# Attention masks moved from TensorE to GpSimd, and exact rounding moved next to its use, in a fused attention and mixture-of-experts kernel

## The chip, the cores and the metric

The kernel runs on one core of one Trainium2 chip. Five engines work side by side, each through its own queue in order: TensorE (PE in the profile; PEld is its weight loads), VectorE (DVE), ScalarE (ACT), GpSimd (POOL) and SyncE (SP, which here only issues DMAs). The metric is the device time of one execution in microseconds (us); less is better.

## The reference

`x` has shape (16, 256, 128): 4096 tokens of 128 channels. Everything is float32.

```python
xn = layernorm(x)                                   # eps 1e-5
Q, K, V = (relu(xn @ W + b) for W, b in ...)         # 16 heads of 8
scores = einsum('bqhd,bkhd->bhqk', Qh, Kh) / sqrt(8)
key_mask = sign(abs(sum(xn, -1)))                   # 0 where the row's sum is exactly 0
scores = where(key_mask == 0, NEG, scores)
scores = where(tril == 0, NEG, scores)              # causal
attn = softmax(scores) * query_mask                 # query_mask is key_mask for the rows
attn_out = gamma * norm(attn @ Vh + xn) + beta      # LayerNorm, eps 1e-8
h = rms_weight * xn * rsqrt(mean(xn**2) + 1e-6)
top 2 of softmax(h @ gate_w.T) over 8 experts, weights normalised to 1
moe = xn + sum over the two of weight * (w2 @ (silu(w1 @ h) * (w3 @ h)))
return x + attn_out + moe
```

The key mask asks whether a row of `xn` sums to exactly zero in float32. So the kernel has to round the quotient `(x - mean) / root` exactly as the reference does; this is what is called exact rounding below.

## The kernel before, in words

128 tokens lie in the 128 partitions of a tile; 32 such tiles form 8 blocks of 4 (`BT = 4`), a block being two sequences. The instructions of TensorE stand in the order in which the program issues them; those of the other engines are put in order by a scheduler, within what their data allow, and keep that order on the chip.

**Early work** (`prepared`, L1059) runs over three chunks of tokens: tiles 0 to 4, 4 to 16, 16 to 32. For each chunk `normed` (L317) makes the LayerNorm: subtract the mean on ACT (L325), square and scan on DVE (L332, L334), a Newton square root in small DVE steps, and `xn` on ACT (L361). `exact` (L385) then rounds block by block: it splits `xn` in a high and a low half (`qh` on DVE, `ql`), makes three products `p` on ACT (L407), adds them to a remainder `r` (L412, L417), corrects `y` (L421), sums each row in the reference's order (`lane_sum`), and writes `off_all` (1 where the row's sum is zero) and `on_all`. For the first chunk the additions run on DVE, for the others on POOL (`eng`). `logits` and `route` (L432) choose two experts a token and scatter rows and weights into `lists` by indirect DMAs from POOL (L536): 32 for the first route (tiles 0 to 16), 16 for each of two more. `planned` (L819) makes the table of expert tiles, 256 tokens each.

**Attention** runs over 16 units: 8 blocks times 2 groups of 8 heads (`r`). `projected(n)` (L569) makes Q, K and V of a block; `diag` (L579) takes `off_all` into K. For a unit u:

- `scores(u, part)`, three parts: S = Q K on TensorE, a causal mask added by a matmul with `cmask[:, 0]` (L648), the row maximum on DVE (L658, L666).
- `queries(u)`: the maxima are transposed (`top_ps`, L685) and put into the queries: Qs on DVE (L687), Qm on ACT (L690).
- `weights(u, part)`, three parts: W = K Qm, transposed scores less their maximum (L710); the causal mask added by a matmul of the identity with `cmask[:, 1]` (L723); exp on ACT (L731) into `e`.
- `values(u, b)`: O = V e on TensorE (L743, L754), then oT on ACT. `finish(u, b)`: transposed back (`o_ps`, L773), divided by the sums, into `y`.

S, W and the experts' A and G share six PSUM buffers; all other PSUM tiles (O, Y, hT, R, `top_ps`, `o_ps`, q, k, v) share two.

**The experts** (`experts`, L900) run over 36 tiles as a generator with four steps a tile: A and G of the first half (L952); Y of the tile before (L969); A and G of the second half; hT of the next tile and R of the one before, with two indirect DMAs into `places` from POOL (L989).

The loop at L1110 interleaves all this. Between the parts of a unit stands `fill`: up to three steps of early work, the next block's projections, 1.55 expert steps on average from unit 3 on, and a step of `rest` (the second LayerNorm of blocks that are done). It is called six times a unit. In the before kernel `queries(u + 1)` stands behind `values(u, 1)`, and before each block the loop drains early work until the next block is rounded (L1114). Behind the last unit run the expert tiles that are left, the last `rest`, and loads of `places` that are added to `y` and written out.

Of the kernel before, what the change touches and what calls it, by code (L numbers as in the profile page):

```python
# [26 lines left out]
def tile_attention_plus_moe(  # L27
# [55 lines left out]
    EARLY_STEPS, EXPERT_STEPS, EXPERTS_FROM = 3, 1.55, 3  # L83
# [55 lines left out]
    for to, src, eng in ((qb_in, bq, nc.scalar), (kb_in, bk, nc.scalar)):  # L139
# [17 lines left out]
    cmask = const.tile([P, 2, P], BF16, name="cmask")  # L157
    G.memset(cmask, 0.0)
    G.affine_select(
        cmask[:, 0, :], cmask[:, 0, :], [[-1, P]], ALU.is_ge, MASKED, base=0, channel_multiplier=1  # L160
    )
    G.affine_select(
        cmask[:, 1, :], cmask[:, 1, :], [[1, P]], ALU.is_ge, MASKED, base=0, channel_multiplier=-1
# [153 lines left out]
    def normed(t0, t1):  # L317
# [60 lines left out]
        ninv = small.tile([P, nt], F32, tag="ninv", name=f"ninv_{n}")  # L378
        V.reciprocal(ninv, root)
        V.tensor_scalar(ninv, ninv, -1.0, None, ALU.mult)  # L380
        rhi, rlo = high_low(root[:], nt, "quot")
        roots[t0] = rhi, rlo, ninv
        yield

    def exact(c0, t0, t1, eng):  # L385

        rhi, rlo, ninv = roots[c0]
        n = f"x{t0}"  # L390
        for b in range(t0, t1, BT):
            bs = slice(b, b + BT)
            q, d = xn[:, bs, :], y[:, bs, :]
            i0 = b - c0
            qh = norm.tile([P, BT, C], F32, tag="qh", name=f"qh_{b}")
            ql = norm.tile([P, BT, C], F32, tag="ql", name=f"ql_{b}")
            r = norm.tile([P, BT, C], F32, tag="r", bufs=2, name=f"r_{b}")
            V.tensor_scalar(
                qh.bitcast(U32), q.bitcast(U32), HI_BITS, None, ALU.bitwise_and
            )  # L400
            eng.tensor_tensor(ql, q, qh, ALU.subtract)
            ps = []
            for k, (half, by) in enumerate(((qh, rlo), (ql, rhi), (ql, rlo))):
                p = norm.tile([P, BT, C], F32, tag=f"p{k}", name=f"p{k}_{b}")
                for t in range(BT):
                    i = i0 + t
                    S.activation(p[:, t, :], half[:, t, :], AF.Copy, scale=by[:, i : i + 1])  # L407
                ps.append(p)
            yield
            for t in range(BT):  # L410
                i = i0 + t
                V.scalar_tensor_tensor(  # L412
                    r[:, t, :], qh[:, t, :], rhi[:, i : i + 1], d[:, t, :], ALU.mult, ALU.subtract
                )
            yield
            for p in ps:
                eng.tensor_tensor(r, r, p, ALU.add)  # L417

            for t in range(BT):
                i = i0 + t  # L420
                V.scalar_tensor_tensor(  # L421
                    d[:, t, :], r[:, t, :], ninv[:, i : i + 1], q[:, t, :], ALU.mult, ALU.add
                )
            yield
        tot = small.tile([P, t1 - t0], F32, tag="tot", name=f"tot_{n}")
        yield from lane_sum(tot, y[:, t0:t1, :], t1 - t0, f"s{n}", V)
        V.tensor_scalar(off_all[:, t0:t1], tot, 0.0, None, ALU.is_equal)
        V.tensor_scalar(on_all[:, t0:t1], off_all[:, t0:t1], -1.0, 1.0, ALU.mult, ALU.add)
        exact_upto[0] = t1 // BT
        yield  # L430
# [138 lines left out]
    def projected(n):  # L569
# [6 lines left out]
        diag = qkv.tile([P, BT, P], BF16, tag="diag", name=f"diag_{n}")  # L576
# [4 lines left out]
        for r in range(NR):  # L581
            kp = misc(f"k_ps_{n}_{r}")
            T.matmul(kp, lhsT=wk_sb[:, r, :], rhs=xnT, start=True, stop=False)
            T.matmul(
                kp,
                lhsT=off_rows,
                rhs=diag.rearrange("p t k -> p (t k)"),
                start=False,
                stop=True,
            )  # L590
            KT = qkv.tile([P, BW], F32, tag="KT", bufs=3, name=f"KT_{n}_{r}")
            S.activation(KT, kp, AF.Relu, bias=kb_sb[:, r : r + 1])

            KTm = qkv.tile([P, HG, BW], F32, tag="KTm", bufs=2, name=f"KTm_{n}_{r}")
            V.tensor_scalar(KTm[:, 0, :], KT, head_mask[:, 0:1], None, ALU.mult)
            S.activation(KTm[:, 1, :], KT, AF.Copy, scale=head_mask[:, 1:2])
            yield
            qp = misc(f"q_ps_{n}_{r}")
            T.matmul(qp, lhsT=wq_sb[:, r, :], rhs=xnT, start=True, stop=True)
            QT = qkv.tile([P, BW], F32, tag="QT", bufs=2, name=f"QT_{n}_{r}")  # L600
            S.activation(QT, qp, AF.Relu, bias=qb_sb[:, r : r + 1], scale=QSCALE)
            state[n, r] = (QT, KT, KTm)
            yield
        for b in range(2):
# [16 lines left out]
    def scores(u, part):  # L621
# [21 lines left out]
        for g in range(NG):  # L643
            if part == 2:
                out = sp[g].rearrange("p (a k) -> p a k", k=P)
            else:
# [4 lines left out]
                rhs=cmask[:, 0, :].unsqueeze(1).to_broadcast([P, 4 if part == 2 else 2, P]),  # L651
# [5 lines left out]
            if part == 2:  # L657
                V.tensor_reduce(  # L658
# [5 lines left out]
                )  # L664
            else:
                V.tensor_reduce(  # L666
# [5 lines left out]
                )  # L672
# [20 lines left out]
    exps = {}  # L693

    def weights(u, part):
# [6 lines left out]
        for g in range(NG):  # L702
            rows = slice(32 * g, 32 * g + 32)
            for b in range(2) if part == 0 else (part - 1,):
                if part == 0:
                    out = sp[g][:, ts(b, SEQ)].rearrange("p (j q) -> p j q", j=HG)
                else:
# [7 lines left out]
                    stop=False,  # L715
                    skip_group_check=True,
                )
        for g in range(NG):
            if part == 0:
                out = sp[g].rearrange("p (a q) -> p a q", q=P)  # L720
            else:
                out = sp[g].rearrange("p (j q) -> p j q", j=HG)[:, :, 0:P]
            T.matmul(  # L723
                out,
                lhsT=ident_bf,
                rhs=cmask[:, 1, :].unsqueeze(1).to_broadcast([P, 4 if part == 0 else 2, P]),
                start=False,
                stop=True,
                skip_group_check=True,
            )  # L730
            S.activation(e[:, g, :], sp[g], AF.Exp)  # L731
# [327 lines left out]
    def prepared():  # L1059

        routed = 0
        for a, z in CHUNKS:
            eng = V if a == 0 else G
            yield from normed(a, z)

            first = min(a + BT, z) if a < 2 * BT else a
            if first > a:
                yield from exact(a, a, first, eng)
# [10 lines left out]
            for b in range(first, z, 2 * BT):  # L1079
                yield from exact(a, b, min(b + 2 * BT, z), eng)  # L1080

    exact_upto = [0]
    early_work = prepared()
    side = {"experts": iter(()), "rest": iter(()), "next": iter(())}
    due = [0.0]

    def fill(k_next=1):

        for _ in range(EARLY_STEPS):
            if next(early_work, None) is PAUSE:  # L1090
                break
        for _ in range(k_next):
# [12 lines left out]
    for _ in projected(0):  # L1105
        pass
# [3 lines left out]
    for u in range(len(units)):  # L1110
        n, r = units[u]
        more = u + 1 < len(units)
        if r == 0 and n + 1 < NB:
            while exact_upto[0] < n + 2:  # L1114
                next(early_work)
            side["next"] = projected(n + 1)
# [3 lines left out]
        fill()  # L1120
        if more:
            if r == 1:
                while (units[u + 1]) not in state:
                    next(side["next"])
            scores(u + 1, 0)
        fill()
        weights(u, 1)
        fill()
        if more:
            scores(u + 1, 1)  # L1130
        fill(r)
# [3 lines left out]
        fill(r)  # L1135
        weights(u, 2)
        finish(u, 0, o0)
        fill(r)
        if r == 1:
            for _ in side["next"]:  # L1140
                pass
        o1 = values(u, 1)
        if more:
            queries(u + 1)
        exps.pop((u, 0))
        finish(u, 1, o1)
# [91 lines left out]
```

## Time and profile before

| | us |
|---|---|
| median of 3 runs (lowest to highest) | 728.03 (725.95 to 730.34) |
| the profiled execution | 728.52 |
| its span, first to last instruction | 726.7 |
| TensorE busy | 566.6 (78%) |
| VectorE busy | 459.8 (63%) |
| ScalarE busy | 324.2 (45%) |
| GpSimd busy | 251.3 (35%) |
| W masks on TensorE (L723), busy | 41.8 |
| exact rounding's additions on GpSimd (L401, L417), busy | 37.0 |

In lines of groups, the columns are: source line, engine, operation, output <- inputs by the program's names, partitions x elements, count; then busy us and mean ns of one; then the engine's idle time before them and what ended it. In timelines: start, length, engine, line, operation, and in brackets the engine's idle time before it. In tables of stages: busy us of each engine with its number of instructions, the granted TensorE clock as a share of full speed, the share of the DMA engines and GB/s.

### The profile page before, as it was taken

To read this page: it belongs to the slowest core of one execution; us is meant where nothing else is said; L and a number is where in the kernel's file an instruction comes from. 1 tells how busy PE (TensorE), PEld (TensorE's weight loads), DVE (VectorE), ACT (ScalarE), POOL (GpSimd) and SP (SyncE) were. 2 spreads that over 40 slices of the span, in tenths; PEclk is the share of its full clock that TensorE was granted. 3 is DMA by queue.
4 is the path that set the end of the run, shared out by engine and by line. 5 is a ranking of instruction groups with operands and counts; after the bars stand their busy time and mean duration, and the time that the engine had idled before them with its cause. 6 is when DMAs were issued, how large, how long until landed. Compare 5 with 4: busy or idle time off the path is not lost.

```text
span 726.7 us, 10435 instructions
## 1 busy us (share of the span) xinstructions
PE 566.6 (78%) x3387; PEld 339.6 (47%) x3401; DVE 459.8 (63%) x1236; ACT 324.2 (45%) x708; POOL 251.3 (35%) x321
## 2 busy tenths in 40 slices
PE   0128778489587898989898989898989899898950
PEld 0013434244354555655455655565555565566740
DVE  5999878976257776655367736564576564637425
ACT  1557755334431634443444553544364444344310
POOL 8404634268814856521121411221142112213630
PEclk9995558889978999999999999999999999999985
DMA  6000000011160225422132211321222122223319
GB/s 160 1 0 0 1 0 1 0 38 38 44 197 27 76 77 147 129 75 67 40 95 64 68 53 54 104 70 45 69 63 83 53 64 75 81 68 91 105 41 329
DMA packets 40761, 50.82 MB, mean 70 GB/s; under 512 B 5925, under 2 KB 33073, under 8 KB 40705
## 3 DMA queue, kind: packets, MB, share of 16 engines
q1 hardware_dynamic: 32128, 38.11, 18.1%
q0 software_dynamic: 4352, 8.47, 3.6%
q10 hardware_dynamic: 4224, 3.55, 1.6%
q8 instruction: 28, 0.46, 0.3%
q14 instruction: 29, 0.23, 0.1%
HBM read 38.35 MB, written 12.27 MB: 70 GB/s over the span
## 4 chain that ended last, share of the span: by engine, by line
PE 52%; DVE 20%; ACT 8%; POOL 7%; issue 6%; DMA 5%; another core or an unknown queue 0%; DVEq 0%; SPq 0%; POOLq 0%; ACTq 0%
PE A L952 7%; PE Y L969 7%; PE G L952 7%; PE S L635 6%; PE W L710 6%; PE O L743 4%; PE W L723 4%; PE S L648 3%; POOL lists L536 3%; ACT e L731 2%; ACT Qm L690 2%; DVE tops L666 2%; DVE y L421 2%; PE O L754 2%; DVE r L412 2%
## 5 line engine op out<-in xcount | busy, mean ns | idle before, releaser
L989 POOL DMA_INDIRECT places<-fres,frows x72 | 70.5, 979 | 272.1 <-DVE fres L985 234.7
L731 ACT ACTIVATE e<-W 128x512 f32<-128x512 f32 x192 | 99.0, 601 | 64.1 <-PE W L723 64.1
L961 DVE SCALAR_TENSOR_TENSOR th<-th,A 112x512 f32<-112x512 f32 x72 | 49.1, 683 | 93.9 <-ACT th L960 93.9
L666 DVE TENSOR_REDUCE tops<-S 128x2 f32<-128x512 f32 x128 | 79.3, 681 | 20.4 <-PE S L648 20.2
L710 PE MATMUL W<-Qm,KT 32*128 32x512 f32 (+1 forms) x512 | 63.0, 569 | 27.8 <-ACT Qm L690 25.2
L952 PE MATMUL A<-hT,w 128*112 128x256 f32 x288 | 78.2, 395 | 7.9 <-ACT hT L943 6.8
L635 PE MATMUL S<-KTm,QT 32*128 32x256 f32 (+1 forms) x512 | 73.3, 560 | 6.0 <-DVE tops L666 4.9
L952 PE MATMUL G<-hT,w 128*112 128x256 f32 x288 | 75.5, 385 | 0.0
L969 PE MATMUL Y<-hid,w 112*128 112x256 f32 x288 | 70.5, 388 | 0.4 <-DVE hid L963 0.4
L536 POOL DMA_INDIRECT lists<-rows_c,ratu_c x64 | 62.4, 975 | 18.5 <-issue 14.4
L960 ACT ACTIVATE th<-A 112x512 f32<-112x512 f32 x72 | 43.4, 602 | 46.6 <-PE A L952 46.6
L952 PEld LDWEIGHTS A<-hT,w 128*112 128x112 f32 x288 | 48.8, 181 | 25.5 <-ACT hT L943 11.0
L969 PEld LDWEIGHTS Y<-hid,w 112*128 112x128 f32 x288 | 54.5, 194 | 11.4 <-issue 1.9
L952 PEld LDWEIGHTS G<-hT,w 128*112 128x112 f32 x288 | 52.0, 181 | 11.8
L764 ACT COPY oT<-O 128x512 f32<-128x512 f32 x32 | 18.8, 586 | 78.1 <-PE O L754 78.1
L963 DVE TENSOR_TENSOR hid<-th,G 112x512 f32<-112x512 f32 x72 | 49.4, 686 | 6.5 <-PE G L952 0.6
L710 PEld LDWEIGHTS W<-Qm,KT 32*128 32x128 f32 x512 | 25.5, 200 | 43.9 <-ACT Qm L690 28.8
L635 PEld LDWEIGHTS S<-KTm,QT 32*128 32x128 f32 x512 | 32.5, 196 | 26.3 <-issue 10.9
L417 POOL TENSOR_TENSOR r<-r,p 128x512 f32<-128x512 f32 x21 | 28.1, 1337 | 43.0 <-DVE r L412 19.5
L658 DVE TENSOR_REDUCE tops<-S 128x4 f32<-128x512 f32 x64 | 39.7, 682 | 3.7 <-PE S L648 3.6
L723 PE MATMUL W<-cmask,ident_bf 128*128 128x256 bf16 (+1 forms) x192 | 41.8, 346 | 0.0
L743 PE MATMUL O<-e,vstat 128*32 128x512 f32 x256 | 38.0, 619 | 2.0 <-ACT hT L943 0.8
(240 smaller groups left out, 880.9 us busy)
## 6 DMA issues: line engine op xcount, KB each, us to landing
w<-in_w1T_dram SPq DMA_DIRECT2D x36, 224.0 KB, 2.6
w<-in_w3T_dram SPq DMA_DIRECT2D x36, 224.0 KB, 3.5
w<-in_w2T_dram SPq DMA_DIRECT2D x36, 224.0 KB, 3.5
frows<-lists SPq DMA_DIRECT2D x36, 130.0 KB, 2.0
x<-in_x_dram SPq DMA_DIRECT2D x8, 256.0 KB, 4.0
z<-places ACTq DMA_DIRECT2D x4, 512.0 KB, 9.4
z<-places SPq DMA_DIRECT2D x4, 512.0 KB, 10.2
lists<-filling SPq DMA_DIRECT2D x9, 130.0 KB, 4.1
```

What stands on the lines that cost most here:

```text
L536: ins = G.indirect_dma_start(out=lists, out_offset=bass.IndirectOffsetOnAxis(ap=at_u[:, r, b + t : b + t + 1], axis=0), in_=rows[:, t, :], ...
L635: T.matmul(out, lhsT=QT[rows, q0 : q0 + P], rhs=KTm[rows, :, b * SEQ : b * SEQ + nk], start=(part < 2 or b == 0), stop=False, skip_group_c ...
L666: V.tensor_reduce(top[:, part, 1, cols], sp[g].rearrange("p (j k) -> p j k", j=HG), AX.X, ALU.max, negate=True,)
L710: T.matmul(out, lhsT=KT[rows, k0 : k0 + P], rhs=Qm[rows, :, k0 : (b + 1) * SEQ], start=(part > 0 or b == 0), stop=False, skip_group_check= ...
L723: T.matmul(out, lhsT=ident_bf, rhs=cmask[:, 1, :].unsqueeze(1).to_broadcast([P, 4 if part == 0 else 2, P]), start=False, stop=True, skip_g ...
L731: S.activation(e[:, g, :], sp[g], AF.Exp)
L743: T.matmul(op[rows, :], lhsT=v[:, 2 * b, r * NG + g, :], rhs=e0[:, g, :], start=True, stop=False, skip_group_check=True, tile_position=(0, ...
L952: T.matmul(to[:, ts(c, SL)], lhsT=wt[:, 0, ts(2 * k + c, CI)], rhs=hT, start=True, stop=True,)
L961: V.scalar_tensor_tensor(th, th, 1.0, ap, ALU.add, ALU.mult)
L963: V.tensor_tensor(h, th, gp, ALU.mult)
L969: T.matmul(yp, lhsT=w2[:, 0, c, :], rhs=hid[c // 2][:, ts(c % 2, SL)], start=(c == 0), stop=(c == NCI - 1),)
L989: ins = G.indirect_dma_start(out=places, out_offset=bass.IndirectOffsetOnAxis(ap=rows[:, a, C : C + 1].bitcast(U32), axis=0), in_=res[:, a ...
```

## The change

Two things are changed together, and the fills are set anew.

1. The causal mask on W. The matmul with `cmask[:, 1]` (L723) is gone. After each exponential, GpSimd's `affine_select` writes 0 into the masked places of `e`, in place: 512 columns a group in part 0, 256 in parts 1 and 2. `cmask` keeps only the half for S.
2. Exact rounding. `exact(n)` takes one block; its roots lie in tiles that stay. Only block 0 is rounded within the early work; the others form a queue of their own, `masks`, of which a fill takes two steps. All of its additions run on DVE. Its row sum is taken block by block.
3. Order. `beside` issues a step of early work or of `masks` so that its DVE and ACT instructions stand behind the last reduction of scores and the last exponential issued before it. In `projected`, q is made ahead of k. In the loop, `queries(u + 1)` moves ahead of `values(u, 1)`; there are seven fills of 1.65 expert steps, from unit 4 on.

```diff
-    EARLY_STEPS, EXPERT_STEPS, EXPERTS_FROM = 3, 1.55, 3
+    EARLY_STEPS, EXPERT_STEPS, EXPERTS_FROM = 3, 1.65, 4
...
-    def exact(c0, t0, t1, eng):
+    behind = {}
+
+    def exact(n):
...
-            eng.tensor_tensor(ql, q, qh, ALU.subtract)
+        V.tensor_tensor(ql, q, qh, ALU.subtract)
...
-            for p in ps:
-                eng.tensor_tensor(r, r, p, ALU.add)
+        for p in ps:
+            V.tensor_tensor(r, r, p, ALU.add)
...
+        for k, _ in enumerate(lane_sum(tot, d, BT, f"s{n}", V)):
...
         for g in range(NG):
+            ins = S.activation(e[:, g, :], sp[g], AF.Exp).ins
+
             if part == 0:
-                out = sp[g].rearrange("p (a q) -> p a q", q=P)
+                on = e[:, g, :].rearrange("p (a q) -> p a q", q=P)
             else:
-                out = sp[g].rearrange("p (j q) -> p j q", j=HG)[:, :, 0:P]
-            T.matmul(
-                out,
-                lhsT=ident_bf,
-                rhs=cmask[:, 1, :].unsqueeze(1).to_broadcast([P, 4 if part == 0 else 2, P]),
...
-            S.activation(e[:, g, :], sp[g], AF.Exp)
+                on = e[:, g, :].rearrange("p (j q) -> p j q", j=HG)[:, :, 0:P]
+            n_on = 2 * HG if part == 0 else HG
+            G.affine_select(
+                on, on, [[0, n_on], [1, P]], ALU.is_ge, no_weight, base=0, channel_multiplier=-1
+            )
+        behind["ACT"] = ins
...
         for a, z in CHUNKS:
-            eng = V if a == 0 else G
             yield from normed(a, z)
-
-            first = min(a + BT, z) if a < 2 * BT else a
-            if first > a:
-                yield from exact(a, a, first, eng)
+            normed_upto[0] = z // BT
+            if a == 0:
+                yield from exact(0)
...
-            for b in range(first, z, 2 * BT):
-                yield from exact(a, b, min(b + 2 * BT, z), eng)
...
+    masks = chain(*(exact(n) for n in range(1, NB)))
...
+    def beside(work):
+
+        with ExitStack() as order:
+            for ins in behind.values():
+                order.enter_context(tc.issue_after(ins))
+            return next(work, None)
+
-    def fill(k_next=1):
+    def fill(k_next=0, k_masks=2):
 
         for _ in range(EARLY_STEPS):
-            if next(early_work, None) is PAUSE:
+            if beside(early_work) is PAUSE:
                 break
+        for _ in range(k_masks):
+            if exact_upto[0] < normed_upto[0]:
+                beside(masks)
...
         o0 = values(u, 0)
-        fill(r)
+        if r == 0 and n + 1 < NB:
+            while exact_upto[0] < n + 2:
+                beside(masks if normed_upto[0] > n + 1 else early_work)
+            side["next"] = projected(n + 1)
+        fill(due_next[4])
         weights(u, 2)
         finish(u, 0, o0)
-        fill(r)
-        if r == 1:
-            for _ in side["next"]:
-                pass
-        o1 = values(u, 1)
         if more:
             queries(u + 1)
+        fill(due_next[5])
+        o1 = values(u, 1)
         exps.pop((u, 0))
+        fill(due_next[6])
         finish(u, 1, o1)
```

## The prediction

> **What bounds the kernel now.** I read the table of stages first (busy time in windows cut at the starts of the units of attention), then the waits, then the timeline of TensorE and GpSimd. A unit starts at its first W matmul: units 0 to 5 at 80.6, 136.7, 167.3, 189.2, 244.5 and 286.2 us, unit 15 at 635.0; its last transpose ends at 660.2.
>
> ```profile
> PE   0128778489587898989898989898989899898950
> DVE  5999878976257776655367736564576564637425
> POOL 8404634268814856521121411221142112213630
> PEclk9995558889978999999999999999999999999985
> ```
>
> The page's 40 slices of 18 us. Up to slice 15 (about 280 us) TensorE (PE) is not full, VectorE (DVE) is at 7 to 9, and the granted clock falls to half; from there on TensorE is at 8 or 9.
>
> ```profile
> core 0: us, PE busy (x) PEld busy (x) DVE busy (x) ACT busy (x) POOL busy (x), PEclk, DMA share, GB/s
> 80.60:136.70 56.10, 39.58 (x179) 19.71 (x180) 47.29 (x116) 30.59 (x84) 24.80 (x19) 0.71 0.00 1
> ...
> 286.20:635.00 348.80, 319.73 (x2061) 192.55 (x2070) 200.62 (x459) 163.18 (x322) 80.06 (x78) 0.98 0.26 74
> 635.00:660.20 25.20, 22.68 (x149) 15.06 (x150) 9.55 (x22) 11.71 (x23) 3.88 (x4) 1.00 0.28 79
> 660.20:701.80 41.60, 37.09 (x169) 29.29 (x167) 22.91 (x55) 14.50 (x31) 19.33 (x18) 0.96 0.24 74
> ```
>
> Units 5 to 14 take 34.9 us each and TensorE is busy for 32.0 of them: it is the bound, with 2.9 us idle a unit. Unit 0 takes 56 us, with DVE busy for 47 of them. Behind the last unit stand 41.6 us that are TensorE's too: the expert tiles that are left.
>
> ```profile
> POOL rows_c L528 <- DVE rwts_c L517: 40.6, 3, 22.9
> PE W L710 <- ACT Qm L690: 25.2, 15, 6.0
> PE hT_ps L941 <- DMA frows<-lists: 7.8, 1, 7.8
> ```
>
> The waits (total, times, longest). 15 times the next unit's W waits for its Qm; between 286 and 635 us it is 15.1 us in all, half of TensorE's idle time there.
>
> ```profile
> 533.89 1.17 PE L710 MATMUL W<-Qm,KT 32*128 32x256 f32 x16 [1.37 <-ACT Qm L690]
> 535.00 1.04 PE L723 MATMUL W<-cmask,ident_bf 128*128 128x512 bf16 x4
> 535.87 0.60 PE L573 MATMUL xnT_ps<-ident,xn 128*128 128x128 f32 x4
> ```
>
> ```profile
> 149.35 0.45 POOL L528 COPY rows_c<-rwts_c 128x4 f32<-128x4 f32 x3 [14.97 <-DVE rwts_c L517]
> 149.97 1.24 POOL L536 DMA_INDIRECT lists<-rows_c,ratu_c  x1 [0.16 <-POOL rows_c L528]
> 151.51 0.96 POOL L536 DMA_INDIRECT lists<-rows_c,ratu_c  x1 [0.31 <-issue]
> 152.77 0.96 POOL L536 DMA_INDIRECT lists<-rows_c,ratu_c  x1 [0.30 <-DMA lists<-rows_c,ratu_c]
> ```
>
> Timelines. A mask group on W moves the next matmul by 0.87 us (535.00 to 535.87) at full clock, less than its 1.04 us of busy time. On GpSimd (POOL) an indirect DMA recurs every 1.26 us, so a route's 32 fill the engine from 149.4 to 198 us.
>
> ```profile
> L417 POOL TENSOR_TENSOR r<-r,p 128x512 f32<-128x512 f32 x21 | 28.1, 1337 | 43.0 <-DVE r L412 19.5 <-ACT p L407 18.1 <-DVE lacc_sx L290 4.9
> masks.py:199 POOL TENSOR_SCALAR_AFFINE_SELECT ident<-ident 128x128 f32<-128x128 f32 x1 | 0.3, 284 | 0.0
> L203 POOL MEMSET keep<- 128x512 f32 x1 | 0.5, 518 | 0.0
> ```
>
> Groups on POOL: the rows that bound the new instruction.
>
> **The change, part by part.** The terms are steps of the profiled execution: span 726.7 us and 1.8 us around it (728.5, against a median of 728.0).
>
> *Masks off TensorE.* 64 groups of 4 and 128 half as wide go. A unit loses 0.87 + 0.45 + 0.44 = 1.76 us of TensorE (starts 535.00 to 535.87, 545.34 to 545.79, 560.88 to 561.33 and their like). Over units 5 to 14: -17.6 us.
>
> *Queries moved ahead of values.* Qm is now made while TensorE does an expert fill, O and another fill, some 6 us, against 0.7 (Qs) + 1.3 (Qm). The wait goes: -15.1 us there. What is late next: with `top_ps` right behind `o_ps`, hT of the experts stands on ACT behind Qm. In four of the ten units a hT step follows there, and the A behind it waits up to 2 us. Bounds 0 and +10; I take +5.
>
> *More expert steps.* Seven fills of 1.65 make 11.55 steps a unit, not 6 of 1.55 = 9.3. A tile has four steps and takes 0.3 + 3.5 + 1.7 + 0.3 = 5.8 us of TensorE, 1.45 a step: 2.25 x 1.45 = +3.26 a unit, +32.6 in ten. Sum for units 5 to 14: -17.6 - 15.1 + 5 + 32.6 = +5; with exps that end 0.4 us sooner for want of masks and so free their banks, +3.
>
> *The end.* 146 steps are to be done. Before, 13 units x 9.3 = 121 are issued by the end of attention; after, 12 x 11.55 = 139. The last unit grows by 2.25 steps and a hT wait less its masks, 25.2 to 29. Behind it two tiles stand instead of six: 13 us of TensorE for 41.6. But the last blocks' LayerNorm (newton, ACT, four POOL operations of 1.28 us between two indirect DMAs) needs some 20 us behind the last unit and had been covered; it now sets the end. So 66.5 us from the last transpose to the end become about 40, 91.7 become 69: -23. Bounds -28 (tiles alone) and -18.
>
> *Rounding on DVE.* 7 `ql` and 21 `r` additions move from POOL (1.27 and 1.34 us) to DVE (0.68): +19 us on DVE, -37 on POOL. In units 5 to 14 DVE is at 200.6 of 348.8, and the rounding of the last block stands in unit 4, so it is nothing there; in units 0 to 4 it counts.
>
> *The front, units 0 to 4.* In the changed program's order on DVE the first block's row sum no longer alternates with seven squares and scans (1.9 us each): the zero flags come at about 37 us (46.5 before), diag, k, KT, KTm and lT add some 7, so S starts at 44 (57.6); S, twelve reductions of 0.68, `top_ps`, Qs and Qm as before put unit 0 at 62 (80.6). From there I add DVE's durations between two units' Qs, in the new order, from the rows of the same lines: 35, 52, 32, 46, 57 us. Overlapped as now (from 46.5 to 77.6 us, 38.7 us of durations took 31.1) they count 0.8: 28, 41, 25, 37, 46, in all 177. That is the lower bound: unit 5 at 62 + 177 + some 12 of start-up waits = 251.
>
> Against it stands POOL's queue. The last exponentials of units 1, 3 and 4 are zeroed behind 16 indirect DMAs of a route (20.2 us, with rows and copies 26 to 29), and unit 2's first ones behind 15 more (30 with its rows); and who waits for them is O, then the unit's end. Unit 1's Qs at 91, its routing weights 40 us of durations x 0.8 behind it, with waits at 125, its O at 151, unit 2 at 154; unit 2's O at 181; then its last exponential stands on ACT behind 16 `xn` and 12 `p` operations (8 us), unit 3 at 198; route 2's weights at 214 (20 us of DVE's order behind the last p), O at 241, unit 4 at 245 (as before, but without unit 3's 9.3 expert steps); route 3's at 266 (21 us of DVE's order into the unit), O at 295, unit 5 at 298. Chained thus with no overlap it is the upper side, +12 us, and +23 if the affine select costs what a two-input operation does. I take 292, nearer to the chain than to DVE alone, because each of its links is an order that is fixed: +6. The experts start in unit 4, long after route 1 is written, so the 7.8 us wait for `frows` goes; nothing is late in its place, for unit 3 no longer holds any expert step. SP's loads for the tiles move back with them.
>
> *The affine select itself.* A square one took 0.28 us; a fill of 512 wide took 0.52, a two-input operation 1.34. For 512 wide I take 0.65 (bounds 0.52 and 1.34), for 256 0.42: 64 x 0.65 + 128 x 0.42 = 95 us, 5.9 a unit. POOL is at 80 of 348.8 us there: room enough. The latency of one, 0.4 us, is on the path before O; 4.6 us of TensorE work stand between W and O, against 3 to 3.6 for four exponentials and the select. Free, unless `places` DMAs (2.5 us a tile) stand ahead: that is part of the +5. Behind a select that waits for its exponential stand other `places` DMAs, which nobody reads before the end. The mask table's second half goes from the start-up: 0.28 us of POOL that nothing waits for.
>
> A rule speaks against it. The Trainium skill, "GPSIMD Engine Reference", section 4.1, keeps elementwise work off GpSimd: about 2 times slower for two inputs, near line rate for one. The row for two inputs is 1.34 us against DVE's 0.68. If the select cost the two-input price, POOL would still have room, but the selects would trail the exponentials (0.5 us apart) by some 1.5 us a unit, and the sum would be 15 us longer.
>
> Sum: 726.7 + 6 + 3 - 23 = 712.7, with 1.8 around it 714.5: forecast 715 us.
>
> **The rivals.** Half a percent, about what a measurement here can tell from no change, is 3.6 us.
>
> - *Only DVE bounds the front.* Unit 5 at 251 to 275: for it, DVE's share in slices 1 to 9; against it, POOL's full slices 8 to 10, and that the selects must pass them. At -18 for the front: 691.
> - *TensorE's freed time turns into waits.* The misc tiles of PSUM are two buffers that O, Y, hT, R, `top_ps` and `o_ps` share, and now follow each other more closely; units of 36.2 instead of 35.2: +10, 725 to 728, no change.
> - *Slower: POOL's queue.* Three routes hold O as in the chain, with selects at the two-input price: unit 5 at 309, +23, and +8 in later units, 738. It decides from a front of +20 on, where the tail's 23 and the steady units' +3 are eaten up.
> - *The masks were hidden.* Not here: TensorE is the bound from 286 us on.
>
> **How the numbers follow.** Chances: forecast 0.42 (front within 12 us of mine, units within 0.6: 700 to 726), DVE alone 0.22, no gain 0.16, POOL's queue 0.20. Faster: nearly all of the first (0.40), the second, and a little of the third: 0.64. Same: 0.02 + 0.09 + 0.02 = 0.13. Slower: 0.23. The range reaches to the rivals on both sides, 690 to 738; the likeliest case's own is 700 to 726.
>
> **What would show it.** Right: unit 0 at about 62 us; no W wait for Qm beyond 3 us; units 5 to 14 at 35 to 35.5 us; 25 us or less from the last O to the last R; O waiting for POOL in units 1 to 4, with indirect DMAs ahead of the selects. Wrong: unit 5 before 275 or after 305; selects above 1 us; a steady unit above 36 us with waits for hT, for `e` from POOL or for misc banks.

## The result and the profile after

The changed kernel takes 762.48 us (760.56 to 766.35) against 729.15 us of the kernel before: a ratio of 1.046, interval 1.043 to 1.050. The forecast was 715, its range 690 to 738. The profiled execution took 766.35 us, its span is 764.6.

The page's slices (busy tenths, 19.1 us each):

```profile
PE   0276694185574647898999799999997899998840
DVE  4856899277687498365646763675467546653545
POOL 8302113886327537422432453243224332533360
PEclk9997686675577768899999989999998999999975
```

TensorE has new holes in slices 7 to 15, and the granted clock is at 5 to 8 from slice 4 to 17. There are smaller holes at slices 23 and 31. The stages (busy us of each engine, clock, share of the DMA engines, GB/s) are, first, units 0 to 4, then units 5 to 14, the last unit, and what stands behind it:

```profile
core 0: us, PE busy (x) PEld busy (x) DVE busy (x) ACT busy (x) POOL busy (x), PEclk, DMA share, GB/s
60.22:319.48 259.26, 164.21 (x816) 86.00 (x819) 189.71 (x621) 111.84 (x279) 126.94 (x177) 0.71 0.13 40
319.48:694.10 374.62, 344.53 (x2105) 213.68 (x2113) 223.47 (x489) 173.99 (x349) 135.40 (x196) 0.97 0.27 77
694.10:723.90 29.80, 25.68 (x150) 17.01 (x150) 11.74 (x30) 12.43 (x25) 11.56 (x18) 0.94 0.21 62
723.90:764.60 40.70, 10.23 (x48) 7.64 (x46) 19.93 (x52) 6.20 (x14) 13.59 (x12) 0.65 0.47 164
```

Set beside the forecast (first W of each unit, us):

| | before | forecast | after |
|---|---|---|---|
| unit 0 | 80.6 | 62 | 60.2 |
| unit 1 | 136.7 | not given | 102.6 |
| unit 2 | 167.3 | 154 | 157.7 |
| unit 3 | 189.2 | 198 | 211.1 |
| unit 4 | 244.5 | 245 | 260.3 |
| unit 5 | 286.2 | 292 | 319.5 |
| units 5 to 14 | 348.8 | 352 | 374.6 |
| last unit | 25.2 | 29 | 29.8 |
| last transpose to end | 66.5 | 40 | 40.7 |

Against the kernel before, 33.3 us are lost in the front and 25.8 in units 5 to 14, and 21.2 are won in the last unit and the tail: 37.9, the difference of the spans (764.6 - 726.7). The end came as forecast; the other two did not.

*The front.* The waits of TensorE in units 0 to 4 (total, times, longest):

```profile
PE O L756 <- POOL e L741: 36.4, 3, 17.0
PE pos_ps_c L491 <- DVE rmine_c L477: 14.7, 3, 5.7
```

The timeline of unit 1 shows the first of the three waits of O (ACT, then POOL with ten DMAs left out, then PE):

```profile
133.89 2.06 ACT L734 ACTIVATE e<-W 128x512 f32<-128x512 f32 x4 [0.49 <-PE W L725]
...
134.07 0.96 POOL L541 DMA_INDIRECT lists<-rows_c,ratu_c  x1 [0.30 <-issue]
...
150.41 0.96 POOL L541 DMA_INDIRECT lists<-rows_c,ratu_c  x1 [0.30 <-issue]
151.37 1.13 POOL L741 TENSOR_SCALAR_AFFINE_SELECT e<-e 128x256 f32<-128x256 f32 x3
...
151.85 3.35 PE L756 MATMUL O<-e,vstat 128*32 128x512 f32 x7 [17.01 <-POOL e L741]
```

The exponentials are done at 135.95. The first of their selects starts at 151.37, when the last of 16 indirect DMAs has ended. O was forecast at 151. The other two waits, 7.7 and 11.7 us, are in units 2 and 3; ahead of unit 2's selects two additions of the second LayerNorm stand as well. The selects cost what was assumed, 0.64 and 0.44 us (0.65 and 0.42 assumed, 93 us in all); it is their place in the queue that costs:

```profile
L741 POOL TENSOR_SCALAR_AFFINE_SELECT e<-e 128x256 f32<-128x256 f32 x128 | 53.8, 435 | 123.7 <-ACT e L734 119.2
L741 POOL TENSOR_SCALAR_AFFINE_SELECT e<-e 128x512 f32<-128x512 f32 x64 | 39.2, 639 | 106.6 <-ACT e L734 106.6
```

*The steady units.* Seven of the ten average 35.5 (forecast 35.2). Unit 5 takes 39.8, which was not followed, and units 8 and 12 stand out. The table of stages, units 8, 9 and 12:

```profile
431.02:471.43 40.41, 34.96 (x206) 21.54 (x206) 25.22 (x61) 19.42 (x40) 18.93 (x24) 0.92 0.26 75
471.43:506.99 35.56, 34.42 (x218) 21.34 (x218) 22.03 (x48) 17.97 (x37) 10.83 (x18) 1.00 0.26 78
576.47:622.72 46.25, 38.39 (x213) 22.93 (x213) 28.28 (x63) 19.72 (x40) 18.75 (x24) 0.89 0.23 68
```

Units 8 and 12 have a lower clock and more work on DVE and POOL: in them the second LayerNorm (`rest`) of two finished blocks runs. Its place follows from its data, so it starts when unit 7 or 11 ends. The timeline at the start of unit 12, POOL, then DVE, then PE:

```profile
579.88 1.29 POOL L1049 TENSOR_TENSOR xn<-xn,beta_sb 128x512 f32<-128x512 f32 x1
581.10 0.65 POOL L741 TENSOR_SCALAR_AFFINE_SELECT e<-e 128x512 f32<-128x512 f32 x1
581.70 1.28 POOL L1050 TENSOR_TENSOR xn<-xn,x 128x512 f32<-128x512 f32 x1
582.92 1.22 POOL L741 TENSOR_SCALAR_AFFINE_SELECT e<-e 128x512 f32<-128x512 f32 x2
...
579.34 1.87 DVE L259 TENSOR_SCALAR l_s<-lv 128x8 uint32<-128x8 uint32 x1
581.25 2.93 DVE L260 TENSOR_SCALAR l_s<-l_s 128x8 uint32<-128x8 uint32 x1
...
586.62 0.68 DVE L974 SCALAR_TENSOR_TENSOR th<-th,A 112x512 f32<-112x512 f32 x1
...
587.35 2.05 PE L965 MATMUL A<-hT,w 128*112 128x256 f32 x4 [4.46 <-DVE th L974]
589.19 1.92 PE L965 MATMUL G<-hT,w 128*112 128x256 f32 x4
591.04 2.00 PE L725 MATMUL W<-Qm,KT 32*128 32x512 f32 x8
```

Two short steps of the Newton root take 1.87 and 2.93 us; the same step takes 0.17 elsewhere in this trace. They last as long as POOL has an addition or a select running. `th` stands behind the root on DVE, the next A needs the PSUM bank that `th` reads, and TensorE waits 4.46 us. Afterwards it runs at half speed until 592.8 (A in 2.05, not 1.03), waits 1.98 us more, and falls to half speed again from 596.2 to 599.6.

### The profile page after: what moved, and what is told of

It is laid out like the page before. It is cut to its first block, busy times and chain, and to the rows that moved or that the text cites. A ratio compares the mean times of both kernels' runs of the same rounds, so it can differ in the third digit from the quotient of the medians.

```text
span 764.6 us, 10298 instructions
## 1 busy us (share of the span) xinstructions
PE 565.3 (74%) x3197; PEld 335.0 (44%) x3209; DVE 481.1 (63%) x1303; ACT 321.7 (42%) x708; POOL 310.4 (41%) x484
## 4 chain that ended last, share of the span: by engine, by line
PE 52%; DVE 19%; ACT 9%; POOL 8%; DMA 6%; issue 6%; SPq 0%; DVEq 0%; POOLq 0%
PE A L965 8%; PE Y L982 7%; PE G L965 7%; PE S L648 6%; PE W L725 6%; POOL lists L541 5%; PE O L756 4%; PE S L661 3%; ACT e L734 3%; DVE tops L679 2%; PE O L767 2%; ACT p L405 2%; PE q_ps L585 2%; DMA lists<-rows_c,ratu_c 2%; DMA z<-places 1%
## 5 line engine op out<-in xcount | busy, mean ns | idle before, releaser
L741 POOL TENSOR_SCALAR_AFFINE_SELECT e<-e 128x256 f32<-128x256 f32 (+1 forms) x192 | 93.0, 503 | 230.3 <-ACT e L734 225.8
L965 PE MATMUL A<-hT,w 128*112 128x256 f32 x288 | 82.6, 412 | 22.6 <-ACT hT L956 10.1
L965 PE MATMUL G<-hT,w 128*112 128x256 f32 x288 | 81.8, 411 | 0.0
L756 PE MATMUL O<-e,vstat 128*32 128x512 f32 x256 | 44.4, 684 | 39.4 <-POOL e L741 36.4
L541 POOL DMA_INDIRECT lists<-rows_c,ratu_c x64 | 64.8, 1012 | 18.2 <-issue 14.2
L725 PE MATMUL W<-Qm,KT 32*128 32x512 f32 (+1 forms) x512 | 69.6, 563 | 2.3 <-ACT Qm L704 2.1
L965 PEld LDWEIGHTS A<-hT,w 128*112 128x112 f32 x288 | 49.8, 186 | 45.6 <-ACT hT L956 13.7
L965 PEld LDWEIGHTS G<-hT,w 128*112 128x112 f32 x288 | 55.5, 193 | 13.8 <-DVE hid L976 0.2
L648 PEld LDWEIGHTS S<-KTm,QT 32*128 32x128 f32 x512 | 34.1, 206 | 27.4 <-DVE tops L679 8.7
L661 PE MATMUL S<-cmask,ident_bf 128*128 128x256 bf16 (+1 forms) x192 | 39.9, 335 | 0.0
L725 PEld LDWEIGHTS W<-Qm,KT 32*128 32x128 f32 x512 | 28.5, 197 | 21.3 <-issue 10.3
```

Of the source, the lines that this page charges most:

```text
L541: ins = G.indirect_dma_start(out=lists, out_offset=bass.IndirectOffsetOnAxis(ap=at_u[:, r, b + t : b + t + 1], axis=0), in_=rows[:, t, :], ...
L648: T.matmul(out, lhsT=QT[rows, q0 : q0 + P], rhs=KTm[rows, :, b * SEQ : b * SEQ + nk], start=(part < 2 or b == 0), stop=False, skip_group_c ...
L661: T.matmul(out, lhsT=ident_bf, rhs=cmask.unsqueeze(1).to_broadcast([P, 4 if part == 2 else 2, P]), start=False, stop=True, skip_group_chec ...
L725: T.matmul(out, lhsT=KT[rows, k0 : k0 + P], rhs=Qm[rows, :, k0 : (b + 1) * SEQ], start=(part > 0 or b == 0), stop=(part > 0 or b == 1), sk ...
L741: G.affine_select(on, on, [[0, n_on], [1, P]], ALU.is_ge, no_weight, base=0, channel_multiplier=-1)
L756: T.matmul(op[rows, :], lhsT=v[:, 2 * b, r * NG + g, :], rhs=e0[:, g, :], start=True, stop=False, skip_group_check=True, tile_position=(0, ...
```

## The experiments

E1 to E4 ran on one chip, E5 to E12 on a second, E13 to E15 on a third. For the runs of the result no chip is on record; their times fit the first. The kernel before took 729.3, 760.8 (761.3 in the second set) and 728.6 us on them; of the second chip more below. Where the same kernel ran on two of them, its units from 6 on have the same lengths to a few tenths, except for units 8 and 12 of the changed kernel (40.4 and 39.1, 46.2 and 45.3) and unit 14 of the changed kernel and of the kernel before (36.8 and 35.1, 31.4 and 29.9).

### E1: all masks on TensorE

```diff
+            T.matmul(out, lhsT=ident_bf, rhs=wmask..., start=False, stop=True)
             ins = S.activation(e[:, g, :], sp[g], AF.Exp).ins
-            G.affine_select(on, on, ...)
```

> The changed kernel with the W masks put back on TensorE and no affine select; rounding, order and fills stay changed. Theory 1 (the selects, queued on POOL behind a route's indirect DMAs, hold O): the waits of O for POOL, 17.0 us in unit 1, 7.7 in unit 2 and 11.7 in unit 3, go, and unit 5 starts at about 285 instead of 319.5; a steady unit rises from 35.4 to 37.2 (1.76 of masks), units 8 and 12 fall to 38 to 41; total near 730. Rival (rounding on DVE and its new order make the front long, and the selects only fill the waits): unit 5 stays at 305 or later, total 750 or more.

Measured 732.99 us, 1.005 (1.003 to 1.007). Unit 5 starts at 285.2, as theory 1 said; the waits of O for POOL are gone. Units 8 and 12 take 39.0 and 42.1. So the selects alone cost 34.3 us of front. Unit 12 without selects:

```profile
550.69 0.17 DVE L264 TENSOR_SCALAR l_s<-lv 128x8 uint32<-128x8 uint32 x1
550.90 1.12 DVE L265 TENSOR_SCALAR l_s<-l_s 128x8 uint32<-128x8 uint32 x1
...
555.64 1.12 PE L984 MATMUL A<-hT,w 128*112 128x256 f32 x4 [1.92 <-DVE th L993]
```

The root, from `lv` to `nm`, takes 6.0 us instead of 9.2, and TensorE waits 1.92 instead of 4.46 and keeps its clock. The selects are part of unit 12's loss; the rest is there without them.

### E2: selects from unit 5 on

```diff
+            if u < 5: T.matmul(out, lhsT=ident_bf, rhs=wmask..., ...)
+            if u < 5: continue
             G.affine_select(on, on, ...)
```

> The changed kernel with masks on TensorE in units 0 to 4 and selects on POOL from unit 5 on. Theory 1: front as with all masks on TensorE (unit 5 near 285), units 5 to 15 as changed (374.6 us in all, units 8 and 12 still at 40 and 46), tail as changed: 764.6 - 34 = 731. Rival as above: unit 5 at 305 or later, 750 or more.

Measured 732.60 us, 1.006 (1.003 to 1.008). Unit 5 starts at 285.6; units 5 to 14 take 374.6, last unit and tail 70.5, both as in the changed kernel. The 34 us of the front lie in the selects of units 0 to 4 alone. Against E1, which has no select at all, the later eleven units win nothing by theirs here (732.60 and 732.99): the seven units without `rest` are 7.2 us shorter in sum, units 8 and 12 are 5.5 longer.

### E3: the route's DMAs in smaller portions

```diff
                     tc.add_to_no_dep_group("lists", ins)
-                yield
+                yield PAUSE
...
+        behind["POOL"] = sel
```

> The changed kernel, all selects on POOL, but a fill takes only one step of a route's rows and DMAs, and POOL's early work stands behind the selects issued before it: 8 indirect DMAs at most between two groups of selects, 10 us, not 16. Theory 1: the longest wait of O for POOL falls from 17 us to 6 or less, the sum from 36 to 15 or less, unit 5 starts 15 to 25 us earlier, at 295 to 305, total 740 to 750. If the front is long for another reason, unit 5 stays at 315 to 320 with the waits elsewhere.

Measured 762.74 us, 1.048 (1.043 to 1.053): no gain, where 740 to 750 was expected. Unit 4 starts at 235.3, 25 us sooner than in the changed kernel, and gives most of it back: units 4 and 5 take 75.0 and 49.8 us, and unit 5 starts at 310.2. TensorE's waits, units 0 to 4:

```profile
PE O L757 <- POOL e L741: 22.3, 3, 10.2
PE hT_ps L955 <- DMA frows<-lists: 20.1, 1, 20.1
```

The waits of O fell from 36.4 to 22.3 (15 or less was expected), but the first expert tile waits 20.1 us for its rows. Their load stands in POOL's queue behind the second route's DMAs, which run at much the same time as before (239 to 252.5 us, in the changed kernel 229 to 251), and is issued at 253.8 (252.5 before); unit 4, which needs the rows, starts 25 us sooner and waits. So the wait moved from one reader of POOL's queue to another.

### E4: the kernel before, with the selects

```diff
-            T.matmul(out, lhsT=ident_bf, rhs=cmask[:, 1, :]..., start=False, stop=True)
             S.activation(e[:, g, :], sp[g], AF.Exp)
+            G.affine_select(on, on, ..., no_weight, base=0, channel_multiplier=-1)
```

> The kernel before, with only the masks moved: affine selects on POOL in place of the W masks, rounding and order as before. POOL then holds rounding, route and selects in one queue. Theory 1: the first selects stand behind the additions of rounding and unit 1's last behind 28 indirect DMAs, so the front grows from 286 to 315 to 335; steady units fall by 1.76 each (19 us over 11); total 740 to 755. Rival (the selects alone are harmless, the new order does the harm): front within 5 us of 286, total near 709.

Measured 777.89 us, 1.066 (1.060 to 1.071): worse than either theory gave. The first W of unit 5 comes at 344.4. In units 0 to 4 O waits for the selects eight times, once for 33.6 us (161.1 to 194.7). In that stretch 24 indirect DMAs of the route, with its rows, stand ahead of them; the last of rounding's additions before it ended at 142.9:

```profile
PE O L740 <- POOL e L726: 54.8, 8, 33.6
```

Units 5 to 14 fall by 7.6 us, not 19. The mask half of the change is a loss by itself; the other half makes it smaller.

### E5 and E6: the second LayerNorm spread

E5 is E2 with this edit, E6 the changed kernel with it. The Newton root (`newton_steps`) yields after each iteration.

```diff
-        next(side["rest"], None)
+        beside(side["rest"])
...
-        if r == 0 and n % 2 == 0 and n >= 4:
+        if r == 0 and 4 <= n <= 6:
-            side["rest"] = rest(n - 4, n - 2, ffn_pool)
+            side["rest"] = rest(2 * n - 8, 2 * n - 6, ffn_pool, slow=True)
```

> Selects from unit 5 on, and the second LayerNorm of blocks 0 to 5 put behind the work issued before it, its Newton root cut into five steps in five fills, in units 9 to 14. Theory 2 (units 8 and 12 are long because TensorE waits for th on VectorE behind the Newton chain, then runs at half clock): units 8 and 12 fall from 40.4 and 46.2 to 36 or less, the units that now hold the steps grow by 1 at most, unit 4 loses its Newton too (1 to 4 us): total 732.6 - 14 - 2 + 3 = 716 to 722. Rival (something else in these units, such as the load of x for the LayerNorm or the adds on POOL): the same 15 us turn up in the units that hold the steps, 730 to 735.

> The same on the changed kernel with all its selects. Theory 2: units 8 and 12 at 36 or less (-15), and unit 4 shorter by 2 to 6, because there the LayerNorm's additions and the selects on POOL had stretched VectorE's short operations; total 742 to 748. If POOL's selects alone were behind units 8 and 12, these stay above 40.

E5: 738.23 us, 0.972 of the kernel before on this chip (0.965 to 0.978); E6: 749.44, 0.986 (0.980 to 0.993). In both, unit 8 takes 34.5 to 34.7 and unit 12 37.3, and the units that hold the steps grow by about 1. E5's units 8, 10 and 12:

```profile
413.10:447.80 34.70, 33.48 (x206) 21.11 (x205) 19.42 (x44) 16.50 (x32) 13.88 (x20) 1.00 0.30 90
...
484.40:520.80 36.40, 35.06 (x217) 22.07 (x216) 21.25 (x46) 18.18 (x36) 16.71 (x23) 1.00 0.29 87
554.70:591.90 37.20, 34.44 (x214) 21.22 (x213) 20.80 (x46) 18.18 (x36) 16.27 (x22) 1.00 0.29 85
```

The clock stays at 1.00, and units 5 to 14 take 360.1 (E5) and 359.8 (E6), where the changed kernel takes 369.2 on the same chip (E9): units 8 and 12, 39.1 and 45.3 there, fall by some 12.5 us together, and units 9 and 10 grow by about 1 each. Theory 2 holds, though unit 12 misses the 36 that was expected. What the edit shows is that the place of the second LayerNorm, at the head of these units, is the cause: it moves the root on VectorE and the additions on GpSimd together, and doesn't part them.

The totals can't be set against E2's, as the chip is another; the changed kernel took 764.17 later on this one (E9), some 14 us more than E6. E5 and E6 differ by the selects of units 0 to 4, and these cost 11.2 us here, not 34 (unit 5 starts at 303.2 in E5 and 313.9 in E6).

### E7: queries back behind values

```diff
-        if more:
-            queries(u + 1)
         fill(due_next[5])
         o1 = values(u, 1)
+        if more:
+            queries(u + 1)
```

> Selects from unit 5 on, with queries(u + 1) back behind values(u, 1). If the step on queries was right, W waits 1.4 us for Qm again in each unit (14 us in ten units) and 3 to 5 come back from hT; units 5 to 15 at 384 to 389 instead of 374.6, total 742 to 747. If the freed wait only moved elsewhere: 733 within 3.

Measured 745.07 us, 0.981 (0.974 to 0.988) on the second chip. By units, the ones without `rest` are as in E2: units 6, 7, 9, 10, 11, 13 and 14 sum to 248.4 us, in E2 to 248.2. No wait of W for Qm is listed in units 6 to 14. The wait that the forecast took off for moving the queries is gone with the queries moved back too: the seventh fill, which stands between Qm and the next W, is what is left to cover it (a run without that fill was not made). The total lies in the range for waits that come back (742 to 747), but by luck: E2 did not run on this chip, and units 5 to 14 take 367.5 us, not 384 to 389. Unit 12 takes 41.6 us here and 45.3 in the changed kernel on the same chip (E9), with a wait for `th` of 2.6 us instead of 4.5, so there the queries ahead made it longer.

### E8: experts from unit 3 on

```diff
-    EARLY_STEPS, EXPERT_STEPS, EXPERTS_FROM = 3, 1.65, 4
+    EARLY_STEPS, EXPERT_STEPS, EXPERTS_FROM = 3, 1.55, 3
```

> Selects from unit 5 on, 1.55 expert steps a fill from unit 3 on: 13 units x 10.85 = 141 steps instead of 12 x 11.55 = 139. By 1.45 us of TensorE a step units 5 to 14 fall by 1.0 each (10 us, less what the waits in units 8 and 12 take back), unit 3 grows by 15.7 less what fills idle time, the tail keeps its 40 (the last LayerNorm sets it): total 726 to 734. If a step costs nothing because it fills waits, units 5 to 14 keep their length and unit 3's growth is the whole change: 740 or more.

Measured 739.63 us, 0.971 (0.965 to 0.978) on the second chip. Set beside the changed kernel on the same chip (E9), units 5 to 14 take 361.5 instead of 369.2 us, last unit and tail 58.2 instead of 70.6, unit 3 60.5 instead of 47.9. The expectation's total was for the first chip and can't be compared.

### E9 to E12: together on one chip

E9 is the changed kernel, E10 is E5, E11 is E5 without selects (masks as in E1), E12 is E5 with E8's edit.

> The changed kernel itself, to stand beside the three below on one chip: the last four runs were on another chip than the first four, where the kernel before took 760.8 instead of 729.3, its steady units being the same. On the first chip 1.046 of the kernel before; on the second, where units 1 to 4 of all kernels are longer, about 1.00 (749.4 for the version with the second LayerNorm spread, and 15 more).

> Selects from unit 5 on, second LayerNorm spread, as before. Against the changed kernel: front shorter by 34 on the first chip and 10 on the second, units 8 and 12 by 15: 49 or 25 less. Against the kernel before: 0.985 (718) on the first chip, 0.972 on the second.

> The same without any select: all W masks on TensorE. What the selects are worth where nothing on POOL holds them: by unit lengths 36.2 to 37.5 with masks against 35.6 to 36.1 with selects, 1.0 a unit, so 10 to 12 us longer than with selects from unit 5 on; by the forecast's 1.76 a unit 19; if masks hide in waits, 3 or less.

> Selects from unit 5 on, second LayerNorm spread, 1.55 expert steps a fill from unit 3 on. With 1.65 from unit 4 on, last unit and tail took 71.7 together; with 1.55 from unit 3 on 58.2, units 5 to 14 fell by 13, and units 3 and 4 grew by some 20: 5 to 8 less than with 1.65 from unit 4 on. If units 3 and 4 have no idle TensorE time for these steps, no difference.

| | us | of the kernel before |
|---|---|---|
| E9 | 764.17 | 1.004 (1.002 to 1.007) |
| E10 | 739.35 | 0.966 (0.959 to 0.974) |
| E11 | 749.60 | 0.984 (0.982 to 0.986) |
| E12 | 724.83 | 0.950 (0.946 to 0.955) |

E10 against E9: 24 to 25 us, the total that was expected on this chip, but not by the parts expected. In the profiles unit 5 starts 16.7 us sooner (10 expected) and units 5 to 14 are 9.1 shorter (15 expected).

E11 against E10: 10.3 us; units 5 to 14 take 371.6 and 360.1, so a unit's masks are worth 1.15 us.

E12 against E10: 14.5 us, twice what was expected. In the profiles, which differ by 10.5, units 0 to 4 are 11.0 us longer, units 5 to 14 10.1 shorter (350.0 against 360.1) and the last unit and tail 11.2 shorter. Units 5 to 14 hold 0.7 steps less each, but unit 5 alone gives 6.2 of the 10.1 us; the other nine give 4.0 us for 6.3 steps, 0.64 a step.

### E13 to E15: rounding's additions back on GpSimd

E13 is E12 with this edit, E14 is E12, E15 the kernel before.

```diff
-        V.tensor_tensor(ql, q, qh, ALU.subtract)
+        (V if n == 0 else G).tensor_tensor(ql, q, qh, ALU.subtract)
...
-            V.tensor_tensor(r, r, p, ALU.add)
+            (V if n == 0 else G).tensor_tensor(r, r, p, ALU.add)
```

> Selects from unit 5 on, second LayerNorm spread, experts from unit 3 on, and the additions of exact rounding of blocks 1 to 7 back on GpSimd. If VectorE's queue sets the front: 19 us less on VectorE, of which 0.8 count, so units 0 to 4 are shorter by up to 15, total 710 to 720 where e14 gives 725. If the front is set by chains of waits between the engines, in which an addition of 1.34 us on GpSimd (behind a route's DMAs at that) takes longer than one of 0.68: longer by 5 to 20.

> The same with the additions on VectorE, to stand beside it on one chip: 0.95 of the kernel before on the second chip (725), 0.97 to 0.98 on the first (706 to 714).

> The kernel before with a profile. On the second chip: units 5 to 14 as on the first (34.9 each), the 32 us in units 0 to 4, in stretches in which VectorE, ScalarE and TensorE all stand still without a releaser beside a route's indirect DMAs, as seen in unit 1 of the version with the second LayerNorm spread (11 us). If this chip runs another clock or slower DMAs, the steady units are longer too.

E13: 738.53 us, 1.014 (1.010 to 1.018). E14: 699.05, 0.959 (0.955 to 0.963), the fastest of all. E15: 729.44, one time, a chip like the first. Units 0 to 4 take 268.1 us in E13 and 230.6 in E14, the rest is equal:

```profile
60.20:328.30 268.10, 182.95 (x954) 100.74 (x954) 176.93 (x590) 114.44 (x282) 131.15 (x147) 0.75 0.16 50
```

```profile
60.20:290.80 230.60, 178.49 (x956) 97.97 (x957) 189.32 (x618) 114.35 (x282) 99.22 (x119) 0.79 0.15 48
```

With 12 us less on DVE the front is 37.5 us longer, more than either theory expected. So DVE's queue as such doesn't set it. TensorE's longest waits in E13's front end with Qs on DVE and lT on ACT (3.2 and 3.6 us in E14):

```profile
PE q_ps L604 <- DVE Qs L720: 20.2, 1, 20.2
PE O L789 <- ACT lT L589: 13.3, 1, 13.3
```

Qs comes late because the row sum and the corrections of rounding, ahead of it on DVE, wait for the additions on POOL, and these stand behind a route's indirect DMAs. Before the 20.2 us wait, `p` was done at 281.6, but 16 DMAs run from 281.07 on (the last of them, the additions, then DVE):

```profile
304.26 0.96 POOL L560 DMA_INDIRECT lists<-rows_c,ratu_c  x1 [0.30 <-issue]
305.24 3.95 POOL L435 TENSOR_TENSOR r<-r,p 128x512 f32<-128x512 f32 x3
309.23 0.35 DVE L439 SCALAR_TENSOR_TENSOR y<-r,ninv_c,xn 128x128 f32<-128x128 f32 x1 [17.77 <-POOL r L435]
```

DVE waits for `r` five times in E13's front, 39.5 us in all, and not at all in E14's. So the second theory holds: it is the queue that held the selects, with another reader.

## Why the prediction was wrong, step by step

- **The front: forecast 292, measured 319.5. This step failed.** Its mechanism, O held by selects behind a route's DMAs, is what the traces show; its sum is wrong in two terms. The first is "the lower bound", 251: DVE's durations of five units, 222 us, times 0.8. E1 has the same front without a select, and there DVE is busy for 184.3 us in units 0 to 4, near that product, but the units take 225.6, and unit 5 starts at 285.2. The factor that turns durations into busy time had been taken for the whole time; DVE is busy for 82% of it, and the clock, 0.73 to 0.90 in these units, was left out. The reading "DVE at 7 to 9 up to slice 15" had hidden this: counted from 0, its digits in slices 9 to 11 are 6, 2 and 5, just where POOL's are 6, 8 and 8. The second fault is how the two were joined: the waits for POOL and DVE's time were set up as two bounds with the truth between them. They add up: 285.2 without selects, 34.3 more with them, of which O's waits are 36.4. Even the upper side, 298, was passed by 21.5 us.
- **The chain's links: the first right, the later ones too short.** O of unit 1 at 151 (151.85), unit 2 at 154 (157.7). Unit 2 was 9.4 us longer than its link (44), unit 3 2.2 (47), unit 4 6.2 (53). For unit 4 the link was also wrong in kind: it had O held by route 3's DMAs, and no such wait was measured there. The unit has three waits of TensorE for DVE (`th` 3.5, `rmine` 5.7, `fres` 4.1) and a clock of 0.77, and is as long without selects (60.1 in E1); that the link came near is luck.
- **The second LayerNorm in units 8 and 12: not in the sum at all, 16 us. This step failed too.** The forecast counted `rest` in the tail alone. Before, the same root stood at the start of unit 12 (5 us of DVE at 535 us) and no wait of TensorE came of it; the next block's projections stood in that stretch of TensorE's order. The change moves them back by four fills and adds selects that stretch the root to 9 us. That the place of the second LayerNorm is the cause is shown by E5 and E6; that TensorE waits for `th` behind the root is read from the trace; how much of it the missing projections make was not tried by itself.
- **The masks, 1.76 us a unit: too large.** 1.15 in E11 against E10, 1.0 in E1 against E2. Where the rest of their time went was not followed.
- **Queries moved ahead, -15.1 with +5 for hT: right in size, wrong in cause.** The wait is gone, but E7 shows that it is gone without this step too; the seventh fill is what is left to cover it. Beside that fill the step is worth nothing in the units without `rest`, and in unit 12 it costs; without the fill it was not tried. The +5 was right: the waits of A for hT in units 5 to 14 rose from 1.4 to 6.2 us.
- **Expert steps, 1.45 each: not settled.** E12 against E10 gives 1.44 with unit 5 and 0.64 without it. The units' sum came near all the same: forecast 35.2 each, and the seven without `rest` and without the front's end in unit 5 average 35.5.
- **The end, -23: right** (-21.2). The last R_ps ends 14 us behind the last O, and the second LayerNorm sets the end: its last operation on GpSimd ends at 743.84, and the loads of `places` that follow start at 744.41.
- **Selects at 0.65 and 0.42 us: right**, so the two-input price of the rule weighed there did not come. Of the rivals, POOL's queue is the one that came, with selects at the low price: it had unit 5 at 309, measured 319.5, and it knew nothing of the 16 us in units 8 and 12.
- **The second chip stays open.** There the kernel before takes 761 us and the changed one 764, so that the loss is 0.4% instead of 4.6%. Units from 6 on are nearly equal there. In E12 units 0 to 4 take 257.5 us, and 230.6 in the same kernel on the third chip (E14); in the changed kernel they are hardly longer (unit 5 starts at 323.4, on the first chip at 319.5). E5's trace has in unit 1, beside a route's DMAs, stops of several engines at once that nothing in the profile ends ("remote" is an unknown queue); DVE, then PE:

```profile
138.85 0.17 DVE L822 TENSOR_SCALAR rs<-o_ps 128x16 f32<-128x16 f32 x1 [3.70 <-remote]
139.06 0.25 DVE L829 RECIPROCAL rs<-rs 128x16 f32<-128x16 f32 x1
143.09 0.69 DVE L720 TENSOR_TENSOR Qs<-QT,top_ps 128x512 f32<-128x512 f32 x1 [3.78 <-remote]
...
143.93 1.94 PE L789 MATMUL O<-e,vstat 128*32 128x512 f32 x8 [11.14 <-issue]
```

Every trace of that chip (E5 to E12) has stops of DVE of this kind of 3.5 to 7 us; on the other two none is above 1 us. The kernel before was not profiled there (E15 fell on another), and the cause was not found.

## What to carry to other kernels

Before work is moved to an idle engine, read what stands in its queue at the moments when the result is due: on an engine that was busy for 35% of the time, the selects of five units cost 34 us on the first chip (7 to 11 on the second), because a route's DMAs of 1.26 us stood ahead of three groups of them. Those of the later eleven units, where the queue is short, won 10 once the second LayerNorm was spread (E10 against E11), and nothing clear before that (E2 against E1). Bounds from different engines are to be added where one's wait is no cover for the other, not averaged. When a filler is moved in TensorE's order, look at what short chain on another engine it had been covering.

## What the runs showed of the hardware

Some short operations of VectorE are held up while GpSimd is at work: a 128x8 TENSOR_SCALAR takes 0.17 us alone, 1.12 us beside one addition of 1.29 (E1), 2.93 beside a select, an addition and two more selects back to back. Not all are: a RECIPROCAL of the same shape kept its 0.20 us beside an addition (unit 8, at 435.37). The Trainium skill, "GPSIMD Engine Reference", section 1, says that GpSimd shares its SBUF interfaces with VectorE and contends with VectorE's two-port modes and two-input instructions. The trace agrees in that GpSimd's work holds VectorE up, and shows that a run of GpSimd instructions without a gap can hold one VectorE instruction for more than one of them; in which mode these instructions ran, no run shows.

The granted clock of TensorE falls to half after a long gap. In unit 8 of the changed kernel it is at half from 439.2 to 446.0 (gap of 4.18 us, matmuls again from 440.32), in unit 12 from 586.0 to 592.8 (gap of 4.46, matmuls again from 587.35): 5.7 and 5.5 us of matmuls at half speed. The Trainium skill, "TensorE: Matmul & The Clock Gate", Part 1, has full speed back after some 3.4 us of sustained work; here it took 1.6 times that. A gap of 1.98 us in unit 12 was followed by half speed from 596.2 to 599.6, one of 1.92 in E1 (555.64) by none, so these runs give no length of gap from which on the clock falls. Unit 12 is 10.8 us longer than the plain units. The two waits (4.46 and 1.98) and half of the matmul time at half speed (5.5 and 3.4) sum to 10.9, an estimate from these numbers.
